# Scans of the first image: products in one PSUM tile, decays in SBUF three steps ahead, and activations taken four in a row from five banks

## Chip, core and metric

The kernel runs on one core of one Trainium2 chip. The metric is the time of one execution on the device in microseconds, as the median of several runs. The engines that matter are TensorE (PE), VectorE (DVE), ScalarE (ACT), GpSimd (POOL) and SyncE (SP), which here only issues DMAs. Each works through its own queue of instructions in order, and semaphores make one wait for another.

## What is computed

Two layers on an input of 4 images with 64 x 64 positions and 128 channels. The first normalises the input and runs a selective state-space layer over each image in three orders (forward, backward, and in 16 interleaved slices). The second is attention with 16 heads of 8 channels, a small feed-forward, and 64 experts, each with its top 8 tokens. The change touches the first layer alone:

```
x, z = split(in_proj(x))                      # 256 channels each
x = silu(causal_conv1d(x, conv_w, conv_b))    # 4 taps
dt_raw, B, C = split(x_proj_w @ x)            # 8, 16, 16 rows
delta = softplus(dt_w @ dt_raw + dt_b)
for each position:                            # the scan, one state for each channel and n < 16
    h = h * exp(delta * A) + (delta * x) * B
    y = sum over n of h * C
y = (y + D * x) * silu(z)
```

## The kernel before

All data is float32. The sequence of an image (4096 positions) is cut into 4 chunks of T = 1024. For an image, an order and a chunk, class Inputs makes what the scan reads, and class Scans scans it. A scan step works on one tile of 128 x 1024: 16 channels by 8 states on the partitions, positions along the row. A chunk has 256 channels by 16 states, so 32 steps, and an image 3 x 4 x 32 = 384.

**Inputs.** For one chunk, `of_chunk` runs these parts, each with a `yield` at which others get their turn:
- cv (L396): projection and convolution in one, 4 groups of 4 matmuls, each group into one PSUM bank of 512 columns; each followed by a Silu on ACT into u (L400)
- xd (L407): two banks of the projection to dt_raw, B and C, copied by ACT (L409)
- dt (L421): four matmuls into four banks, with Softplus on ACT into r (L427), which is delta
- the product of delta and u, for the early chunks, on POOL (L436)
- the results go to DRAM: u, delta, the product, B and C, by DMAs on SP.

`gate` (L352, L358) makes Silu(z) of a quarter of an image in the same way. The `norm` of an image loads and transposes x (L302), copies it (L304), takes statistics on DVE (L307) and normalises (L328). These share three banks: `bank` hands one out and waits, by yielding, while three are held; `leave` gives one back.

**Scans.** Step s of `of_image`: `load(s)` brings delta and du (the product of delta and x, broadcast over the states; one tile serves two steps), B, C and u. delta has three tiles and is loaded by SP, du has four and, for image 0, is loaded from ACT's queue. `exp(s)` (L525) computes the decay exp(delta A) on ACT, and `inputs(s)` (L532) the product of du with B on DVE. `step(s)` runs the scan on DVE (L542), has POOL copy its last column for the next chunk (ends, L544) and, for image 0, multiply with C (hC, L549); for later images DVE does that. `total` (L580) adds over the states on PE, for a group of four steps at a time, and `out` (L596) adds D x on DVE from the one bank `y`.

For image 0 (`alone`) the loads run four steps ahead of the step, the decay one step and the product two. Its decays lie in two PSUM tiles of two banks each; its products in three SBUF tiles. So PSUM's 8 banks go to the decays (4), Inputs (3) and y (1).

**Order of the work around the change.** While image 0 is scanned, the inputs of all four images are made. The order on every engine is the order in which the program issues, set by hand:

```
first = Pace(decays(nc, dirs, ws, inputs), scans.of_image(0, inputs.made, True))
others = Pace(flow(inputs.pieces(range(nb)), 2, 10))
while not first.done:
    others.run(1.2)
    first.run(1.0)
others.rest()
```

`Pace.run(x)` advances its generator to x more yields. A scan step has two yields, so 2.4 yields of the others fall on one. `flow` keeps up to two pieces (a chunk, a gate, a norm) in progress, advances them in turn, and starts another when the last has come 10 yields far. Afterwards the attention of image 0 begins, beside the scans of image 1.

Of the kernel before, what the change touches and what calls it, by code (L numbers as in the profile page):

```python
# [11 lines left out]
F32 = mybir.dt.float32  # L12
AF = mybir.ActivationFunctionType
# [3 lines left out]
P = 128  # L17
# [4 lines left out]
NS = 16  # L22
R = 8
SLICES = 16
ORDERS = {0: (0, 1, 2), 1: (1, 2, 0)}
T = 1024
NC = L // T
# [206 lines left out]
class Inputs:  # L234
# [3 lines left out]
    def __init__(self, tc, ctx, x, w_z, ws, cols, dram, ident):  # L238
        nc = self.nc = tc.nc
        self.x, self.w_z, self.ws, self.cols, self.dram, self.ident = x, w_z, ws, cols, dram, ident  # L240
        const = ctx.enter_context(tc.tile_pool(name="i_const", bufs=1))
        self.big = ctx.enter_context(tc.tile_pool(name="i_big", bufs=1))
        self.piece = ctx.enter_context(tc.tile_pool(name="i_piece", bufs=1))
        self.small = ctx.enter_context(tc.tile_pool(name="i_small", bufs=2))
        self.ps = ctx.enter_context(tc.tile_pool(name="i_ps", bufs=3, space=PSUM))

        group = const.tile([P, 32, 4], F32, name="group")
        nc.gpsimd.memset(group, 0.25)
        nc.gpsimd.affine_select(
            out=group, in_=group, compare_op=ALU.is_ge, fill=0.0,  # L250
            base=0, pattern=[[-4, 32], [0, 4]], channel_multiplier=1,
        )
        nc.gpsimd.affine_select(
            out=group, in_=group, compare_op=ALU.is_ge, fill=0.0,
            base=3, pattern=[[4, 32], [0, 4]], channel_multiplier=-1,
        )
        self.group = group.rearrange("p g r -> p (g r)")
        self.made, self.sz, self.normed, self.sliced, self.gated = {}, {}, {}, {}, {}
        self.held = 0

    def bank(self, name):
        while self.held == 3:
            yield WAIT
        self.held += 1
        return self.ps.tile([P, 512], F32, tag="a", name=name)

    def leave(self):
        self.held -= 1
# [75 lines left out]
    def gate(self, b, g):  # L344
        nc, xn = self.nc, self.normed[b]
        s_g = self.piece.tile([P, 2, T], F32, tag="u", bufs=2, name=f"z_{b}_{g}")
        for m in range(2):
            banks = []
            for i in range(T // 512):
                ps = yield from self.bank(f"z_{b}_{g}_{m}_{i}")  # L350
                at = 3 + g * T + i * 512
                nc.tensor.matmul(  # L352
                    ps, self.w_z[:, m * P : (m + 1) * P], xn[:, at : at + 512], start=True, stop=True,
                )
                banks.append(ps)
            yield
            for i, ps in enumerate(banks):
                nc.scalar.activation(s_g[:, m, i * 512 : (i + 1) * 512], ps, AF.Silu)  # L358
                self.leave()
        yield  # L360
        yield
        nc.sync.dma_start(out=self.sz[b].rearrange("(m p) t -> p m t", p=P)[:, :, g * T : (g + 1) * T], in_=s_g)
        self.gated[b] += 1
        yield

    def of_chunk(self, b, order, c):
# [21 lines left out]

        halves = [slice(g * 512, (g + 1) * 512) for g in range(T // 512)]
        u = self.piece.tile([P, 2, T], F32, tag="u", bufs=2, name=f"u_{key}")  # L390
        for m in range(2):
            bias = w["conv_b"][:, m : m + 1]
            for g, cut in enumerate(halves):
                ps = yield from self.bank(f"cv_{key}_{m}_{g}")
                for k in range(4):
                    nc.tensor.matmul(  # L396
                        ps, w["conv"][:, k, m * P : (m + 1) * P], reads(k, g), start=(k == 0), stop=(k == 3)
                    )
                yield
                nc.scalar.activation(u[:, m, cut], ps, AF.Silu, bias=bias)  # L400
                self.leave()
        yield
        xd = self.piece.tile([X_ROWS, T], F32, tag="xd", name=f"xds_{key}")
# [7 lines left out]
        keep("u", u)  # L411
        yield
        r = self.piece.tile([P, 2, T], F32, tag="r", name=f"r_{key}")
        for m in range(2):
            banks = []
            for g in range(2):
                banks.append((yield from self.bank(f"dt_{key}_{m}_{g}")))
            for g, cut in enumerate(halves):
                at = 32 * (2 * m + g)
                rows = slice(at, at + R)  # L420
                nc.tensor.matmul(banks[g], w["dt"][rows, m, :], xd[rows, cut], start=True, stop=True)  # L421
            if m == 0:
                nc.sync.dma_start(out=made["bc"][0], in_=xd[B_ROW : B_ROW + NS])
                nc.sync.dma_start(out=made["bc"][1], in_=xd[C_ROW : C_ROW + NS])
            yield
            for g, cut in enumerate(halves):
                nc.scalar.activation(  # L427
                    r[:, m, cut], banks[g], AF.Softplus, bias=w["dt_proj_b"][:, m : m + 1]
                )
                self.leave()  # L430
        yield
# [14 lines left out]
class Scans:  # L446
# [24 lines left out]
    def of_image(self, b, made, alone=False):  # L471
# [45 lines left out]
        def exp(s):  # L517
            order, c, k, j = steps[s]
            t = tiles["delta", s]
            if alone:  # L520
                tiles["delta", s] = self.ps.tile([P, T], F32, tag="dA", name=f"dA_{b}_{s}")
            elif j % 2 == 0:
                tiles["delta", s] = self.deep.tile([P, T], F32, tag="dA", bufs=2, name=f"dA_{b}_{s}")
            A = self.ws[order]["A"][:, j % 2, 2 * k + j // 2].unsqueeze(1)
            nc.scalar.activation(tiles["delta", s], t, AF.Exp, scale=A)  # L525

        def inputs(s):
            order, c, k, j = steps[s]
            du = tiles["du", s]
            if alone or j % 2 == 0:  # L530
                tiles["du", s] = self.deep.tile([P, T], F32, tag="dB", bufs=3, name=f"dB_{b}_{s}")
            nc.vector.tensor_mul(tiles["du", s], du, spread[order, c, "B", j % 2])  # L532

        def step(s):
# [8 lines left out]
            if c < NC - 1:  # L543
                nc.gpsimd.tensor_copy(ends[order, c][:, at : at + 1], h[:, T - 1 :])  # L544
            if alone:
                if s + 2 < n:
                    inputs(s + 2)
                tiles["du", s] = self.lone.tile([P, T], F32, tag="hC", bufs=5, name=f"hC_{b}_{s}")
                nc.gpsimd.tensor_mul(tiles["du", s], h, spread[order, c, "C", j % 2])  # L549
                return  # L550
# [81 lines left out]
        if b == 0:  # L632
            for w in self.ws:
                nc.scalar.activation(w["A"], w["A"], AF.Exp)
                nc.vector.tensor_scalar_mul(w["A"], w["A"], -1.0)
        exp(0)
        for s in range(2 if alone else 1):
            inputs(s)
        y = None

        def sums(s):
# [10 lines left out]
        for s in range(n):  # L652
# [7 lines left out]
                y = self.bank.grab(f"y_{b}_{s}")  # L660
            if s + ahead < n:
                load(s + ahead)
            if s + 1 < n:
                exp(s + 1)
                self.did.add("exp")
            if turn in (1, 2):
                sums(s)
# [834 lines left out]
def tile_kernel(tc, ctx, x, in_proj_w, dirs, out_proj_w, attn, gate, weight1, weight2, out):  # L1502
# [15 lines left out]
    with ExitStack() as fill:  # L1518
# [6 lines left out]
        inputs = Inputs(tc, fill, x, w_z, ws, cols, dram, ident)  # L1525
        scans.bank = Bank(fill.enter_context(tc.tile_pool(name="s_bank", bufs=1, space=PSUM)), 1)
        scans.lone = fill.enter_context(tc.tile_pool(name="s_lone", bufs=1))
        scans.ps = fill.enter_context(tc.tile_pool(name="s_ps", bufs=2, space=PSUM))
        with tc.manual_schedule():
            first = Pace(decays(nc, dirs, ws, inputs), scans.of_image(0, inputs.made, True))  # L1530
            others = Pace(flow(inputs.pieces(range(nb)), 2, 10))
            while not first.done:
                others.run(1.2)
                first.run(1.0)
            others.rest()
    bank = scans.bank = Bank(ctx.enter_context(tc.tile_pool(name="bank", bufs=1, space=PSUM)), 1)
# [115 lines left out]
```

## Time and profile before

| what | value |
|---|---|
| median of 3 runs | 11542.6 us (11537.03 to 11542.7) |
| the profiled execution | 11539.8 us, of which the span is 11538.0 us |
| busy in the span: PE, DVE, ACT, POOL | 87%, 71%, 89%, 33% |
| mean granted clock of PE in the span | 0.935 |
| first scan of image 0 starts, last one ends | 113.8 us, 1941.9 us |
| matmul cv (L396), all | 1536 instructions |
| decays of image 0 (L525), mean in 113 to 1824 us | 1117 ns |
| products of image 0 (L532), mean in 113 to 1824 us | 1316 ns |
| hC (L549), all 384 | 976.8 us busy, mean 2544 ns |

A matmul of 128 x 512 in float32 stands in the profile as two instructions, so cv's 768 matmuls are 1536. The lines of the profile name the source line, the engine, the operation and what is written and read; "mean" is that of one instruction, and the time after the bar's second part is the engine's idle time just before, with what ended it. Idle time is put down to the semaphore that is seen last. Where an instruction waits for several semaphores, a separate wait in the sequencer can hide the true cause, and "issue" then stands in its place. A table load (ACT_TABLE_LOAD) is the change of ACT's set of functions, which Exp, Silu and Softplus each need.

### The profile page before, as it was taken

To read this page: it belongs to the slowest core of one execution; us is meant where nothing else is said; L and a number is where in the kernel's file an instruction comes from. 1 tells how busy PE (TensorE), PEld (TensorE's weight loads), DVE (VectorE), ACT (ScalarE), POOL (GpSimd) and SP (SyncE) were. 2 spreads that over 40 slices of the span, in tenths; PEclk is the share of its full clock that TensorE was granted. 3 is DMA by queue.
4 is the path that set the end of the run, shared out by engine and by line. 5 is a ranking of instruction groups with operands and counts; after the bars stand their busy time and mean duration, and the time that the engine had idled before them with its cause. 6 is when DMAs were issued, how large, how long until landed. Compare 5 with 4: busy or idle time off the path is not lost.

```text
span 11538.0 us, 182909 instructions
## 1 busy us (share of the span) xinstructions
PE 10009.7 (87%) x68358; PEld 3314.4 (29%) x68358; DVE 8174.7 (71%) x8379; ACT 10305.7 (89%) x11065; POOL 3770.4 (33%) x3917
## 2 busy tenths in 40 slices
PE   7787784488999889999998898999998999999995
PEld 3233332122222222222222222222222223333323
DVE  5777777788888987998898978988988421111212
ACT  5687784599999999999999999999999999989992
POOL 5776666232322312424333224233332110000000
PEclk8788886799999999999999999999999999999997
DMA  6777777656665665566565656655556332222225
GB/s 188 213 231 204 210 213 202 178 138 154 152 150 146 174 190 138 158 159 149 145 155 148 181 170 161 155 144 144 149 144 170 125 94 71 70 78 83 75 65 184
DMA packets 900977, 1747.50 MB, mean 151 GB/s; under 512 B 203150, under 2 KB 443846, under 8 KB 899830
## 3 DMA queue, kind: packets, MB, share of 16 engines
q1 hardware_dynamic: 764734, 1469.68, 47.0%
q0 software_dynamic: 93856, 156.41, 4.8%
q10 hardware_dynamic: 41496, 109.71, 3.5%
q8 instruction: 537, 8.80, 0.3%
q14 instruction: 354, 2.90, 0.1%
HBM read 1379.76 MB, written 355.47 MB: 150 GB/s over the span
## 4 chain that ended last, share of the span: by engine, by line
PE 34%; ACT 23%; issue 14%; DVE 7%; DMA 6%; POOL 1%; SPq 1%; ACTq 0%; DVEq 0%; POOLq 0%
PE acc L992 20%; ACT e L983 20%; PE s L978 9%; DVE h L542 2%; DMA du<-d_du 1%; DMA delta<-d_delta 1%; ACT dA L525 1%; PE fo L1149 1%; ACT delta L525 1%; PE h L1136 1%; DMA w<-in_L_ffn_weight_dram 1%; DVE dB L532 1%; PE y L580 1%; DMA y<-d_y 0%; DVE du L553 0%
## 5 line engine op out<-in xcount | busy, mean ns | idle before, releaser
L983 ACT ACTIVATE e<-s 128x1024 f32<-128x1024 f32 x8192 | 7778.9, 1106 | 231.1 <-PE s L978 193.2
L992 PE MATMUL acc<-e,val 128*32 128x512 f32 x32768 | 5250.0, 616 | 105.5 <-ACT av L1001 91.6
L978 PE MATMUL s<-qm,key 32*128 32x512 f32 x16384 | 2652.0, 501 | 587.0 <-ACT e L983 556.6
L978 PEld LDWEIGHTS s<-qm,key 32*128 32x128 f32 x16384 | 1013.2, 184 | 4448.6 <-issue 2493.7
L544 POOL COPY ends<-h 128x1 f32<-128x1 f32 x1152 | 1264.9, 1099 | 2501.6 <-DVE h L542 2486.2
L542 DVE TENSOR_TENSOR_SCAN h<-dA,ends,dB 128x1024 f32<-128x1024 f32 x720 | 1687.6, 2344 | 337.2 <-issue 205.7
L532 DVE TENSOR_TENSOR dB<-du,B 128x1024 f32<-128x1024 f32 x960 | 1197.0, 1247 | 408.0 <-PE y L580 221.2
L992 PEld LDWEIGHTS acc<-e,val 128*32 128x32 f32 x32768 | 971.3, 109 | 1603.1 <-issue 788.8
L525 ACT ACTIVATE dA<-delta,A 128x1024 f32<-128x1024 f32 x960 | 1143.4, 1193 | 221.9 <-DVE h L542 131.3
L542 DVE TENSOR_TENSOR_SCAN h<-delta,ends,du 128x1024 f32<-128x1024 f32 x432 | 1012.1, 2343 | 132.1 <-ACT delta L525 65.4
L549 POOL TENSOR_TENSOR hC<-h,C 128x1024 f32<-128x1024 f32 x384 | 976.8, 2544 | 146.8 <-DVE h L542 73.0
L525 ACT ACTIVATE delta<-delta,A 128x1024 f32<-128x1024 f32 x576 | 717.2, 1245 | 0.1
L553 DVE TENSOR_TENSOR du<-h,C 128x1024 f32<-128x1024 f32 x576 | 700.9, 1217 | 0.1
L553 DVE TENSOR_TENSOR dB<-h,C 128x1024 f32<-128x1024 f32 x576 | 700.8, 1217 | 0.0
L532 DVE TENSOR_TENSOR du<-du,B 128x1024 f32<-128x1024 f32 x576 | 690.5, 1199 | 5.3 <-DMA B<-d_bc 5.2
L542 DVE TENSOR_TENSOR_SCAN h<-dA,dB 128x1024 f32<-128x1024 f32 x240 | 548.4, 2285 | 123.1 <-issue 69.8
L1007 POOL DMA_DIRECT2D d_ctx<-av x512 | 260.3, 518 | 1013.9 <-DVE av L1001 645.1
L396 PE MATMUL cv<-xn,conv 128*128 128x512 f32 x1024 | 499.4, 644 | 32.3 <-DVE xn L328 32.3
L574 POOL DMA_DIRECT2D d_du<-x_delta x272 | 157.2, 578 | 1012.1 <-DVE x_delta L573 950.2
L580 PE MATMUL y<-dB,sel 128*32 128x256 f32 x4608 | 376.7, 399 | 9.9 <-DVE xT L1176 6.2
L580 PE MATMUL y<-hC,sel 128*32 128x256 f32 x3072 | 255.5, 467 | 144.7 <-DVE o L596 139.6
L542 DVE TENSOR_TENSOR_SCAN h<-delta,du 128x1024 f32<-128x1024 f32 x144 | 328.8, 2283 | 68.5 <-issue 35.4
(244 smaller groups left out, 7248.8 us busy)
## 6 DMA issues: line engine op xcount, KB each, us to landing
delta<-d_delta SPq DMA_DIRECT2D x768, 512.0 KB
du<-d_du SPq DMA_DIRECT2D x576, 512.0 KB
du<-d_du ACTq DMA_DIRECT2D x192, 512.0 KB
key<-d_q SPq DMA_DIRECT2D x352, 256.0 KB
d_u<-u SPq DMA_DIRECT2D x48, 1024.0 KB
d_delta<-r SPq DMA_DIRECT2D x48, 1024.0 KB
B<-d_bc SPq DMA_DIRECT2D x96, 512.0 KB
C<-d_bc SPq DMA_DIRECT2D x96, 512.0 KB
```

What stands on the lines that cost most here:

```text
L396: nc.tensor.matmul(ps, w["conv"][:, k, m * P : (m + 1) * P], reads(k, g), start=(k == 0), stop=(k == 3))
L525: nc.scalar.activation(tiles["delta", s], t, AF.Exp, scale=A)
L532: nc.vector.tensor_mul(tiles["du", s], du, spread[order, c, "B", j % 2])
L542: nc.vector.tensor_tensor_scan(h, dA, dB, first, ALU.mult, ALU.add)
L544: nc.gpsimd.tensor_copy(ends[order, c][:, at : at + 1], h[:, T - 1 :])
L549: nc.gpsimd.tensor_mul(tiles["du", s], h, spread[order, c, "C", j % 2])
L553: nc.vector.tensor_mul(dB, h, spread[order, c, "C", j % 2])
L580: nc.tensor.matmul(y[32 * g : 32 * g + 32, : T // 4], self.sel[:, j // 2, :], hC[:, 256 * g : 256 * g + 256], start=(j == 0), stop=(j == 3),)
L978: nc.tensor.matmul(s_ps[:, k, :], keys[f"{i // 4}"][rows, cut].bitcast(F32R), queries[j, qb][rows, :].bitcast(F32R), start=True, stop=True,)
L983: nc.scalar.activation(e, s_ps, AF.Exp, scale=1.0 / math.sqrt(D))
L992: nc.tensor.matmul(accs[j, qb][32 * k : 32 * k + 32, :], v[:, k * VW : k * VW + 32], es[i][k // 2][:, k % 2, :], start=(kc == 0), stop=(kc ...
L1007: nc.gpsimd.dma_start(out=self.context[b][h * D : h * D + D, cut], in_=av[32 * k : 32 * k + D, :])
```

## The change

Of image 0's scans: the product of du with B (L532) goes to one PSUM tile of two banks and is made one step ahead, so just before its scan. The decays go to SBUF: for even steps to three tiles of their own, for odd steps in place of delta's tile, as in later images. Three decays are issued ahead instead of one. This leaves five banks for Inputs.

Of Inputs: a batch of four banks is taken at once, for cv, for dt and for a gate. All matmuls of the batch are issued first, and after a further yield (for a chunk) the four activations in a row. A chunk has one yield more, and the others' pace goes from 1.2 to 1.3.

```diff
+BANKS = 5
-        self.ps = ctx.enter_context(tc.tile_pool(name="i_ps", bufs=3, space=PSUM))
+        self.ps = ctx.enter_context(tc.tile_pool(name="i_ps", bufs=BANKS, space=PSUM))
...
+    def banks(self, n, name):
+        while self.held + n > BANKS:
+            yield WAIT
+        self.held += n
+        return [self.ps.tile([P, 512], F32, tag="a", name=f"{name}_{i}") for i in range(n)]
...
     def gate(self, b, g):
+        banks = yield from self.banks(4, f"z_{b}_{g}")
         for m in range(2):
-            banks = []
-            for i in range(T // 512):
-                ps = yield from self.bank(f"z_{b}_{g}_{m}_{i}")
+            for i in range(2):
...
-            yield
-            for i, ps in enumerate(banks):
-                nc.scalar.activation(s_g[:, m, i * 512 : (i + 1) * 512], ps, AF.Silu)
+            yield
+        for m in range(2):
+            for i in range(2):
+                nc.scalar.activation(s_g[:, m, i * 512 : (i + 1) * 512], banks[2 * m + i], AF.Silu)
                 self.leave()
...
+        banks = yield from self.banks(4, f"cv_{key}")
         for m in range(2):
-            bias = w["conv_b"][:, m : m + 1]
-            for g, cut in enumerate(halves):
-                ps = yield from self.bank(f"cv_{key}_{m}_{g}")
+            for g in range(2):
                 for k in range(4):
...
                 yield
-                nc.scalar.activation(u[:, m, cut], ps, AF.Silu, bias=bias)
+        yield
+        for m in range(2):
+            for g, cut in enumerate(halves):
+                nc.scalar.activation(u[:, m, cut], banks[2 * m + g], AF.Silu, bias=w["conv_b"][:, m : m + 1])
                 self.leave()
...
+        banks = yield from self.banks(4, f"dt_{key}")
         for m in range(2):
-            banks = []
-            for g in range(2):
-                banks.append((yield from self.bank(f"dt_{key}_{m}_{g}")))
             for g, cut in enumerate(halves):
...
-            if m == 0:
-                nc.sync.dma_start(out=made["bc"][0], in_=xd[B_ROW : B_ROW + NS])
-                nc.sync.dma_start(out=made["bc"][1], in_=xd[C_ROW : C_ROW + NS])
-            yield
+        nc.sync.dma_start(out=made["bc"][0], in_=xd[B_ROW : B_ROW + NS])
+        nc.sync.dma_start(out=made["bc"][1], in_=xd[C_ROW : C_ROW + NS])
+        yield
+        yield
+        for m in range(2):
             for g, cut in enumerate(halves):
...
         def exp(s):
-            if alone:
-                tiles["delta", s] = self.ps.tile([P, T], F32, tag="dA", name=f"dA_{b}_{s}")
-            elif j % 2 == 0:
-                tiles["delta", s] = self.deep.tile([P, T], F32, tag="dA", bufs=2, name=f"dA_{b}_{s}")
+            if j % 2 == 0:
+                tag, bufs = ("dB", 3) if alone else ("dA", 2)
+                tiles["delta", s] = self.deep.tile([P, T], F32, tag=tag, bufs=bufs, name=f"dA_{b}_{s}")
...
         def inputs(s):
-            if alone or j % 2 == 0:
+            if alone:
+                tiles["du", s] = self.ps.tile([P, T], F32, tag="dB", name=f"dB_{b}_{s}")
+            elif j % 2 == 0:
...
             if alone:
-                if s + 2 < n:
-                    inputs(s + 2)
+                if s + 1 < n:
+                    inputs(s + 1)
...
-        exp(0)
-        for s in range(2 if alone else 1):
-            inputs(s)
+        further = 3 if alone else 1
+        for s in range(further):
+            exp(s)
+        inputs(0)
...
-            if s + 1 < n:
-                exp(s + 1)
+            if s + further < n:
+                exp(s + further)
...
-        scans.ps = fill.enter_context(tc.tile_pool(name="s_ps", bufs=2, space=PSUM))
+        scans.ps = fill.enter_context(tc.tile_pool(name="s_ps", bufs=1, space=PSUM))
...
-                others.run(1.2)
+                others.run(1.3)
```

More of the change, by code (lines that the diff above doesn't have):

```diff
@@ L259, in __init__ @@
         self.held = 0
+    def banks(self, n, name):
[3 more added lines that the diff above has]
+        return [self.ps.tile([P, 512], F32, tag="a", name=f"{name}_{i}") for i in range(n)]
     def bank(self, name):
[L262 to L265, printed above, removed]
+        return (yield from self.banks(1, name))[0]
     def leave(self):
@@ L346, in gate @@
         s_g = self.piece.tile([P, 2, T], F32, tag="u", bufs=2, name=f"z_{b}_{g}")
+        banks = yield from self.banks(4, f"z_{b}_{g}")
         for m in range(2):
[L348 to L350 removed]
+            for i in range(2):
                 at = 3 + g * T + i * 512
                 nc.tensor.matmul(
[L353 removed]
+                    banks[2 * m + i], self.w_z[:, m * P : (m + 1) * P], xn[:, at : at + 512], start=True, stop=True,
                 )
[L355 removed]
             yield
[L357 to L358 removed]
+        for m in range(2):
+            for i in range(2):
+                nc.scalar.activation(s_g[:, m, i * 512 : (i + 1) * 512], banks[2 * m + i], AF.Silu)
                 self.leave()
@@ L390, in of_chunk @@
         u = self.piece.tile([P, 2, T], F32, tag="u", bufs=2, name=f"u_{key}")
+        banks = yield from self.banks(4, f"cv_{key}")
         for m in range(2):
-            bias = w["conv_b"][:, m : m + 1]
-            for g, cut in enumerate(halves):
-                ps = yield from self.bank(f"cv_{key}_{m}_{g}")
+            for g in range(2):
                 for k in range(4):
                     nc.tensor.matmul(
-                        ps, w["conv"][:, k, m * P : (m + 1) * P], reads(k, g), start=(k == 0), stop=(k == 3)
+                        banks[2 * m + g], w["conv"][:, k, m * P : (m + 1) * P], reads(k, g), start=(k == 0), stop=(k == 3)
                     )
                 yield
-                nc.scalar.activation(u[:, m, cut], ps, AF.Silu, bias=bias)
+        yield
+        for m in range(2):
+            for g, cut in enumerate(halves):
+                nc.scalar.activation(u[:, m, cut], banks[2 * m + g], AF.Silu, bias=w["conv_b"][:, m : m + 1])
                 self.leave()
@@ L420, in of_chunk @@
                 rows = slice(at, at + R)
-                nc.tensor.matmul(banks[g], w["dt"][rows, m, :], xd[rows, cut], start=True, stop=True)
-            if m == 0:
-                nc.sync.dma_start(out=made["bc"][0], in_=xd[B_ROW : B_ROW + NS])
-                nc.sync.dma_start(out=made["bc"][1], in_=xd[C_ROW : C_ROW + NS])
-            yield
+                nc.tensor.matmul(banks[2 * m + g], w["dt"][rows, m, :], xd[rows, cut], start=True, stop=True)
+        nc.sync.dma_start(out=made["bc"][0], in_=xd[B_ROW : B_ROW + NS])
[3 more added lines that the diff above has]
+        for m in range(2):
             for g, cut in enumerate(halves):
                 nc.scalar.activation(
-                    r[:, m, cut], banks[g], AF.Softplus, bias=w["dt_proj_b"][:, m : m + 1]
+                    r[:, m, cut], banks[2 * m + g], AF.Softplus, bias=w["dt_proj_b"][:, m : m + 1]
                 )
```

## Prediction

> **What bounds the kernel now.** I looked for the stage that the change touches before asking what any instruction costs. All edited lines run while image 0 is scanned; in the trace its 384 scan steps (L542) run from 113.8 to 1941.9 us, 1828 us or 4.76 us a step. The view of windows splits that into the part in which other images' inputs are made beside it, and the tail in which the scans run alone.
>
> ```profile
> core 0: us, PE busy (x) PEld busy (x) DVE busy (x) ACT busy (x) POOL busy (x), PEclk, DMA share, GB/s
> 113.00:1824.00 1711.00, 1388.28 (x5238) 541.55 (x5238) 1318.77 (x845) 1338.36 (x1374) 1240.14 (x682) 0.84 0.75 216
> 1836.00:1942.00 106.00, 26.72 (x232) 11.93 (x232) 106.00 (x69) 32.42 (x29) 93.90 (x30) 0.56 0.69 153
> ```
>
> No engine is full in the first part; DVE is full in the tail. So in the first part something waits for something in turn. The groups of that window name it (busy, mean of one, then idle before them):
>
> ```profile
> L542 DVE TENSOR_TENSOR_SCAN h<-dA,ends,dB 128x1024 f32<-128x1024 f32 x256 | 600.4, 2345 | 254.4 <-issue 187.2 <-POOL hC L549 39.5 <-POOL ends L544 19.2
> L525 ACT ACT_TABLE_LOAD x227 | 291.2, 1283 | 23.8 <-DMA delta<-d_delta 11.5 <-DMA du<-d_du 4.4 <-DMA d_y<-o 3.7
> ...
> L542 DVE TENSOR_TENSOR_SCAN h<-dA,dB 128x1024 f32<-128x1024 f32 x96 | 219.4, 2285 | 90.6 <-issue 66.1 <-POOL ends L544 12.8 <-POOL hC L549 8.5
> ...
> L400 ACT ACT_TABLE_LOAD x136 | 174.5, 1283 | 69.7 <-PE cv L396 49.2 <-issue 16.4 <-DMA d_du<-u 2.0
> ...
> L427 ACT ACT_TABLE_LOAD x60 | 77.0, 1283 | 3.1 <-issue 2.1
> ...
> L358 ACT ACT_TABLE_LOAD x31 | 39.8, 1283 | 0.6
> ```
>
> DVE idles 254.4 + 90.6 = 345.0 us in front of the scans, nearly all of its 392 us idle. "issue", hC and ends are poor names for the cause. The timeline shows it:
>
> ```profile
> 917.47 1.28 ACT L525 ACT_TABLE_LOAD   x1
> ...
> 918.76 1.12 ACT L525 ACTIVATE dA<-delta,A 128x1024 f32<-128x1024 f32 x1
> ...
> 919.90 1.28 ACT L358 ACT_TABLE_LOAD   x1
> 920.32 2.35 DVE L542 TENSOR_TENSOR_SCAN h<-dA,ends,dB 128x1024 f32<-128x1024 f32 x1 [1.72 <-issue]
> ```
>
> The decay ends at 919.88 and the scan starts 0.44 us later. Pairing the n-th decay with the n-th scan, 344.6 us of the 345 end with a decay. The decays have two PSUM tiles, so decay s+1 cannot start before scan s-1 ends; it then has 1.2 us (product) + 2.3 us (scan s), and one Silu between costs 1.28 + 0.69 + 1.28 + 1.12 = 4.37 us.
>
> What comes next is in the waits and in the tail:
>
> ```profile
> PE xt L302 <- DMA x<-in_x_dram: 90.9, 12, 17.9
> ...
> PE y L580 <- DVE o L596: 66.7, 21, 12.6
> PE dt L421 <- ACT r L427: 64.9, 36, 4.0
> ...
> DVE stats L307 <- ACT xn L304: 37.3, 16, 7.6
> ```
>
> ```profile
> 1866.42 1.19 DVE L532 TENSOR_TENSOR dB<-du,B 128x1024 f32<-128x1024 f32 x1
> ...
> 1866.64 3.17 POOL L549 TENSOR_TENSOR hC<-h,C 128x1024 f32<-128x1024 f32 x1 [0.66 <-DVE h L542]
> ...
> 1867.53 2.34 DVE L542 TENSOR_TENSOR_SCAN h<-dA,ends,dB 128x1024 f32<-128x1024 f32 x1
> 1869.79 1.19 DVE L532 TENSOR_TENSOR dB<-du,B 128x1024 f32<-128x1024 f32 x1
> ```
>
> PE is 81% busy in the first part, with idle time that other causes set. DVE's own step is 1.11 (1866.42 to 1867.53) + 2.26 = 3.37 us, and the closing operation (L596, 0.49 us) every fourth step.
>
> [...] The trace has the 1283 ns; the decay follows 1.29 us after the load's start and the load 0.02 us after its forerunner, so I count 1.28 us a switch. [...] hC takes 3.17 us beside a product in the tail, 2.35 us beside a scan. [...] The dependent pair L119, L120 starts 0.71 us apart (1999.35, 2000.06), L120 and its independent follower 0.61. [...] The granted mean is 0.84 at 81% busy and 0.56 at 25%.
>
> **The change part by part.**
>
> *Decays three steps ahead, in SBUF.* Decay s+3 is issued at step s, so a decay may be late by about three steps before DVE notices. The worst pair of batches, Silu and Softplus (each 1.28 + 4 x 0.69 + 1.28 = 5.3 us) with two decays, is 13 us against some 11. The 345.0 us go, apart from what is priced below. The decay itself costs more in SBUF: later images' rows give 1.25 us against 1.12, 384 x 0.13 = 50 us of ACT, hidden while ACT has that idle time (below).
>
> *Fewer table loads.* Now 227 + 136 + 60 + 31 = 454, or 582 us. Afterwards 48 Silu batches, 48 Softplus batches and 16 gate batches, at most two loads each: 224. Counting yields, a few batches adjoin: 221. That takes 233 x 1.283 = 299 us from ACT: 1338 - 299 + 50 = 1089 us. ACT stops being a candidate for the bound.
>
> *Products in one PSUM tile, one step ahead.* Each scan directly follows the product that it reads: +0.10 us x 384 = 38 us on DVE. A write to PSUM by DVE is not in the trace. [...] ScalarE's 1.12 against 1.25 us in favour of PSUM, taken whole for DVE, -50 us. I take 0, since scans from PSUM and SBUF decays take the same (2285 ns here, 2283 ns for h<-delta,du of later images). If the overwrite of the tile also waits for the scan in front, another 38 us.
>
> *delta's tile is held until the scan.* Odd decays are written in place, so the load for pair p+2 waits for scan 2p-1 instead of its decay. SP stands there, with the stores, the us loads and the others' x loads and keeps queued behind it. One turn of the three tiles is six steps: load, wait in ACT's queue, a table load and decay (2.4), two scans with the products (5.9), SP's issue (0.6). Counting SP's bytes against its packets, such loads land after 5.7 us in the median, 10.5 at the 95th percentile. At 4.2 us a step, 25.2 - 8.9 = 16.3 us remain for load and queue: hidden in most turns.
>
> *Four banks in a row out of five.* PE can start a batch's first group in the fifth bank and then needs ACT's activations of the batch before. Only one such batch fits, so batches follow one another strictly, 48 + 48 + 16 = 112 of them. The dt waits for banks (64.9) go. In exchange xd waits for Silus that now start late: between 0 and a load and three Silus, 3.3 us, less what of the other piece lies between; I take 1.25 us x 48 = 60.
>
> *Pace 1.3.* A chunk has one yield more. By the yields, the others end at scan step 361 of 384; now 353. So 23 steps are left alone, at 3.37 + 0.10 + 0.12 = 3.6 us: 83 us.
>
> **The sum.** DVE alone would need 1828 - 345 + 38 = 1521 us. PE for the others' part: matmuls of 512 columns start 0.43 us apart at the full clock (LDWEIGHTS of cv at 899.84 and 900.27), 2432 x 0.43 = 1046, y 215, xt 24: 1285 us, against 1388 now. I take about the middle, 1335. To it come waits that stay: x loads 91, xn 30, xd on u 19, dt on xds 15, small ones 3, together 158, and the 60 above: 1553 us, 4.30 us a step. PE and DVE are tied within a few steps (y needs the products with C, o needs y, one bank), so the longer one ends: 1553 + 83 = 1636, 192 us less than 1828. From the profiled execution's 11539.8 us this gives 11348; the median of the runs is 2.8 us higher, so 11350. Later stages shift as they are.
>
> **The rivals.**
>
> *PE takes over (the forecast), 192 us off.* For it: 81% busy already, and 4.21 us a step in the best 16 steps, PE 94% busy. Its range is PE at the full clock without the xd waits, 1285 + 158, so DVE's 1521 ends: 307 off; to PE as slow as now with all waits and 2.5 us at each xd: 1388 + 158 + 120 = 1666, 79 off.
>
> *DVE's own floor, 307 us off, 11235.* For it: POOL and ACT have room. Against: POOL. Its ends and hC need 3.45 us a step, and 26 products u (2.65 us) fall in the first 97 steps: 404 us against DVE's 349.
>
> *The delta ring binds.* If load and queue average 18 us, a step is (18 + 8.9)/6 = 4.5 us, the stage 1728: 100 off, 11443. Against: 5.7 us median.
>
> *Slower: PE stands at each hand-over of the banks.* 112 batches in series; every wait of PE adds to 1553. From 192/112 = 1.7 us a batch on, nothing is gained; at 3.0 us (a load and most of three activations, uncovered) it is 336 - 192 = 144 us slower, 11694. For it: only one spare bank, and three now serve finer grains. Against: cv's first group (8 x 0.43 = 3.4 us) runs in that bank meanwhile, and a decay's delay no longer reaches DVE.
>
> **How the numbers follow.** PE takes over 0.53, DVE floor 0.14, delta ring 0.17, slower 0.11, and 0.05 that the gains and losses cancel. The range reaches from the floor (11235, 11240 taken) to 11500, which takes in the ring at 19 us. Within 0.2% (23 us; about what a measurement of this kernel tells from no change): 0.05; slower 0.11; faster 0.84.
>
> **What would show it.** Right: idle before L542 falls from 345 to below 80 us; table loads number about 221; PE is above 88% busy with a clock above 0.84 in the first part; the last scan ends near 1750. DVE's product-to-scan distance in the tail is 1.2 instead of 1.11 us. Wrong: PE under 80% busy with waits on u or r in front of cv, xd and dt (the bank rival); ACT idle before L525 on delta loads (the ring); scans still late by decays; DVE products longer than 1.2 us.

## The result, and the profile after

| | before | after |
|---|---|---|
| median (lowest to highest) | 11539.82 us (11534.12 to 11542.7), 4 runs | 11420.67 us (11410.54 to 11439.44), 4 runs |
| ratio after/before | | 0.9899, 95% interval 0.9882 to 0.9916 |
| the profiled execution, and its span | 11539.8, 11538.0 us | 11419.52, 11417.8 us |
| first scan of image 0 starts, last ends | 113.8, 1942.0 us | 107.2, 1814.0 us |
| that stage | 1828.2 us | 1706.7 us |
| table loads of ACT in it | 455 | 222 |
| busy in it: PE, DVE, ACT, POOL | 1419, 1429, 1376, 1337 us | 1293, 1577, 1072, 1350 us |

The change takes 119 us off, 1.0%. The stage accounts for it: 121.5 us shorter. The forecast was 11350 us with a range of 11240 to 11500, so direction and range hold and the gain is 119 instead of 192 us.

In the changed kernel the scan is L547, the decay L528, the product L537, hC L554, ends L549, y L585, o L601; of Inputs, Silu into u is L405, Softplus into r L431, xd L412, cv L398. First the windows of after, the part with the others' inputs and then the tail (columns as in the forecast):

```profile
core 0: us, PE busy (x) PEld busy (x) DVE busy (x) ACT busy (x) POOL busy (x), PEclk, DMA share, GB/s
107.20:1740.00 1632.80, 1275.02 (x5349) 509.60 (x5349) 1504.88 (x879) 1050.21 (x1160) 1286.92 (x695) 0.87 0.81 234
1740.00:1814.00 74.00, 18.03 (x161) 8.17 (x161) 71.81 (x49) 21.33 (x20) 62.58 (x19) 0.55 0.54 122
```

DVE is now 92% busy (1504.88 of 1632.80), against 77% before. PE, which was to become the bound, is 78% busy. But DVE's busy time is not all work, as the groups of the stage show (busy, mean of one in ns, then idle before them and what ended it):

```profile
L554 POOL TENSOR_TENSOR hC<-h,C 128x1024 f32<-128x1024 f32 x383 | 983.5, 2569 | 210.4 <-PE y L585 111.6 <-issue 57.4 <-DVE h L547 33.6
L537 DVE TENSOR_TENSOR dB<-du,B 128x1024 f32<-128x1024 f32 x384 | 610.9, 1591 | 23.8 <-DMA du<-d_du 9.6 <-DMA B<-d_bc 1.3
...
L547 DVE TENSOR_TENSOR_SCAN h<-dA,ends,dB 128x1024 f32<-128x1024 f32 x144 | 337.8, 2346 | 20.6 <-ACT dA L528 3.3
L547 DVE TENSOR_TENSOR_SCAN h<-delta,ends,dB 128x1024 f32<-128x1024 f32 x144 | 336.8, 2339 | 15.9 <-ACT delta L528 6.7 <-DVE dB L537 1.0
...
L528 ACT ACTIVATE dA<-delta,A 128x1024 f32<-128x1024 f32 x191 | 219.0, 1147 | 332.0 <-DMA delta<-d_delta 294.5 <-DVE dB L537 14.8 <-DVE h L547 9.8
```

The idle time in front of the scans has shrunk from 345 to 54 us (two groups with 9 us each are left out here); in 19.1 us of it the decay came last. But a product's mean is 1591 ns, where the first part of before had 1316:

```profile
L532 DVE TENSOR_TENSOR dB<-du,B 128x1024 f32<-128x1024 f32 x353 | 464.7, 1316 | 11.9 <-DMA B<-d_bc 7.2 <-DMA du<-d_du 4.7
```

It has not become more work: the median is 1.23 us (1.20 before). 82 of the 384 took over 1.5 us, and what these spent above 1.2 us adds up to 139 us (before: 31 of them, 36 us). All 82 began while POOL was at work: 69, with 115 us, beside an hC, and 13, with 24 us, beside POOL's product of delta and u. Each ends 1.09 us after that instruction of POOL (1.087 to 1.095). The 292 products that began with no POOL instruction under way took 1.235 us at most, so the 1.09 us are nearly a whole product that comes after POOL's instruction. In the profile such a wait has no line of its own: it is counted as duration. I call these products held; "port" in the expectations below is a name for this hold. Why POOL's instruction has this effect was not shown.

Why does hC run just then? The timeline of after, around one held product, and three lines of the tail:

```profile
994.97 1.15 ACT L528 ACTIVATE dA<-delta,A 128x1024 f32<-128x1024 f32 x1 [6.33 <-DMA delta<-d_delta]
996.13 1.28 ACT L405 ACT_TABLE_LOAD   x1
...
998.17 5.54 PE L412 MATMUL xd<-u,w_x 128*104 128x512 f32 x8 [8.15 <-ACT u L405]
...
1002.40 2.35 DVE L547 TENSOR_TENSOR_SCAN h<-delta,ends,dB 128x1024 f32<-128x1024 f32 x1 [2.58 <-ACT delta L528]
1003.64 1.07 PE L585 MATMUL y<-hC,sel 128*32 128x256 f32 x16
1004.45 2.38 POOL L554 TENSOR_TENSOR hC<-h,C 128x1024 f32<-128x1024 f32 x1 [10.31 <-issue]
1004.78 3.13 DVE L537 TENSOR_TENSOR dB<-du,B 128x1024 f32<-128x1024 f32 x1
...
1745.00 2.35 DVE L547 TENSOR_TENSOR_SCAN h<-dA,ends,dB 128x1024 f32<-128x1024 f32 x1
1747.38 1.23 DVE L537 TENSOR_TENSOR dB<-du,B 128x1024 f32<-128x1024 f32 x1
1748.75 2.35 DVE L547 TENSOR_TENSOR_SCAN h<-delta,ends,dB 128x1024 f32<-128x1024 f32 x1
```

Read it downwards. A decay on ACT waits 6.33 us for a load of delta (by the chain of waits it landed 14.2 us after its issue). The Silu batch stands behind it in ACT's queue, so xd on PE waits 8.15 us for u. y stands behind xd on PE, and until y has read a tile of hC, POOL has no tile for the next one: it waits 10.31 us ("issue" again stands for it, but it ends as y's matmuls run). Then hC starts 0.33 us ahead of a product and holds it for 1.9 us. So DVE, with its decays far ahead, still pays for a late ACT, along ACT, PE and POOL. The waits of after give the totals for the same links (us, times, longest):

```profile
ACT dA L528 <- DMA delta<-d_delta: 260.0, 55, 13.4
...
POOL hC L554 <- PE y L585: 111.6, 43, 8.4
...
PE xd L412 <- ACT u L405: 103.8, 23, 26.1
...
PE xt L306 <- DMA x<-in_x_dram: 88.3, 12, 15.2
...
DVE stats L311 <- ACT xn L308: 49.8, 15, 9.5
```

xd's wait on u was 19 us before, hC's on y 52 us. The wait of hC is not all due to xd's: during its 111.6 us PE is at work for 106, 76 of them on matmuls of Inputs that stand ahead of y in its queue. That xd's wait came first, as in the timeline, is shown for this one place.

### The profile page after: what moved, and what is told of

Its sections match the earlier page's. It is cut to its first block, busy times and chain, and to the rows that moved or that the text cites. A ratio compares the mean times of both kernels' runs of the same rounds, so it can differ in the third digit from the quotient of the medians.

```text
span 11417.8 us, 183032 instructions
## 1 busy us (share of the span) xinstructions
PE 9875.8 (86%) x68358; PEld 3273.8 (29%) x68358; DVE 8319.4 (73%) x8379; ACT 9990.1 (87%) x10828; POOL 3815.4 (33%) x3917
## 4 chain that ended last, share of the span: by engine, by line
PE 37%; ACT 23%; issue 14%; DVE 14%; DMA 11%; POOL 1%; SPq 1%; ACTq 0%; DVEq 0%; POOLq 0%
PE acc L998 21%; ACT e L989 19%; PE s L984 10%; DVE h L547 6%; DMA delta<-d_delta 4%; DVE dB L537 2%; DMA du<-d_du 2%; PE cv L398 1%; ACT dA L528 1%; PE y L585 1%; ACT delta L528 1%; PE fo L1155 1%; PE h L1142 1%; DMA B<-d_bc 1%; PE xd L412 1%
## 5 line engine op out<-in xcount | busy, mean ns | idle before, releaser
L549 POOL COPY ends<-h 128x1 f32<-128x1 f32 x1152 | 1298.8, 1129 | 2274.5 <-DVE h L547 2265.9
L537 DVE TENSOR_TENSOR dB<-du,B 128x1024 f32<-128x1024 f32 x960 | 1306.5, 1361 | 426.9 <-PE y L585 225.1
L547 DVE TENSOR_TENSOR_SCAN h<-dA,ends,dB 128x1024 f32<-128x1024 f32 x576 | 1350.6, 2345 | 100.4 <-ACT dA L528 57.5
L528 ACT ACTIVATE dA<-delta,A 128x1024 f32<-128x1024 f32 x768 | 934.4, 1217 | 461.4 <-DMA delta<-d_delta 422.8
L547 DVE TENSOR_TENSOR_SCAN h<-delta,ends,du 128x1024 f32<-128x1024 f32 x432 | 1012.5, 2344 | 124.3 <-ACT delta L528 62.3
L554 POOL TENSOR_TENSOR hC<-h,C 128x1024 f32<-128x1024 f32 x384 | 985.8, 2569 | 210.8 <-PE y L585 111.6
L528 ACT ACTIVATE delta<-delta,A 128x1024 f32<-128x1024 f32 x768 | 936.7, 1220 | 7.1 <-issue 2.0
L537 DVE TENSOR_TENSOR du<-du,B 128x1024 f32<-128x1024 f32 x576 | 690.7, 1199 | 6.4 <-DMA B<-d_bc 6.3
L398 PE MATMUL cv<-xn,conv 128*128 128x512 f32 x1024 | 476.5, 620 | 37.8 <-DVE xn L332 25.6
L547 DVE TENSOR_TENSOR_SCAN h<-dA,dB 128x1024 f32<-128x1024 f32 x192 | 438.7, 2285 | 41.3 <-ACT dA L528 30.1
L585 PE MATMUL y<-dB,sel 128*32 128x256 f32 x4608 | 379.3, 401 | 8.1 <-DVE xT L1182 5.2
L547 DVE TENSOR_TENSOR_SCAN h<-delta,du 128x1024 f32<-128x1024 f32 x144 | 328.8, 2283 | 67.3 <-issue 34.9
L585 PE MATMUL y<-du,sel 128*32 128x256 f32 x4608 | 364.3, 388 | 0.0
```

What stands on the lines that cost most here:

```text
L398: nc.tensor.matmul(banks[2 * m + g], w["conv"][:, k, m * P : (m + 1) * P], reads(k, g), start=(k == 0), stop=(k == 3))
L547: nc.vector.tensor_tensor_scan(h, dA, dB, first, ALU.mult, ALU.add)
L585: nc.tensor.matmul(y[32 * g : 32 * g + 32, : T // 4], self.sel[:, j // 2, :], hC[:, 256 * g : 256 * g + 256], start=(j == 0), stop=(j == 3),)
```

## The experiments

In the order of the questions. Times are medians, each with its ratio to the kernel before on the same chip (that one: 11538.69 us beside e1 to e4, 11540.96 beside e5 to e8, 11552.23 beside e9 to e12). As that kernel moves by up to 14 us between the groups, a smaller difference between runs of two groups says nothing. "Late decays" is DVE's idle time ended by a decay, "held" the time above 1.2 us of all products over 1.5 us, both in the stage. Table loads are counted here from the program's start to the end of the stage, 4 to 6 of them ahead of the first scan in runs with loads. In summary:

| run | us | stage | loads to its end | late decays | held | hC waits for y |
|---|---|---|---|---|---|---|
| before | 11539.8 | 1828.2 | 461 | 344.6 | 35.8 | 52.3 |
| after | 11420.7 | 1706.7 | 226 | 19.1 | 139.4 | 111.6 |
| e1_one_tile | 11556.9 | 1848.8 | 463 | 58.8 | 220.3 | 348.6 |
| e2_two_tiles | 11548.8 | 1830.6 | 463 | 5.1 | 170.6 | 304.4 |
| e4_before_next | 11553.2 | 1844.9 | 463 | 320.9 | 46.6 | 49.2 |
| e9_before_noload | 11425.9 | 1700.6 | 1 | 163.9 | 61.4 | 67.4 |
| e10_one_tile_noload | 11443.7 | 1733.9 | 3 | 10.0 | 169.4 | 202.7 |
| e5_one_decay | 11423.9 | 1714.7 | 226 | 116.2 | 51.7 | 53.3 |
| e3_hc7 | 11397.7 | 1692.5 | 226 | 44.3 | 76.9 | 4.5 |
| e8_ends_dve_hc7 | 11396.1 | 1685.4 | 226 | 41.8 | 72.1 | 24.7 |
| e7_delta5 | 11425.2 | 1713.4 | 226 | 20.5 | 139.1 | 100.2 |
| e6_two_taps | 11382.8 | 1680.0 | 226 | 20.1 | 106.8 | 63.7 |
| e11_norm_ahead | 11359.9 | 1648.5 | 222 | 15.8 | 118.8 | 122.3 |
| e12_norm_u | 11385.7 | 1656.4 | 222 | 12.2 | 48.3 | 103.1 |

**The lead of the decays alone.** The scans of after with the Inputs of before: three banks, one Silu or Softplus at a time, pace 1.2.

```diff
...
-                tiles["delta", s] = self.ps.tile([P, T], F32, tag="dA", name=f"dA_{b}_{s}")
...
+            if j % 2 == 0:
+                tag, bufs = ("dB", 3) if alone else ("dA", 2)
...
+                tiles["du", s] = self.ps.tile([P, T], F32, tag="dB", name=f"dB_{b}_{s}")
...
-                if s + 2 < n:
-                    inputs(s + 2)
+                if s + 1 < n:
+                    inputs(s + 1)
...
-            if s + 1 < n:
-                exp(s + 1)
+            if s + further < n:
+                exp(s + further)
...
```

> The changed kernel's scans (decays in SBUF three steps ahead, products in one PSUM tile one step ahead) with the Inputs of the kernel before (three banks, activations after each bank, pace 1.2). Theory 'order' (the shortfall comes from each product standing right before its scan in one tile): the scans' tail, where DVE runs alone, has 3.81 us a step as in the changed kernel; decays still no longer late (idle before the scans under 60 us); 454 table loads; about 11430 to 11480 us, since ACT keeps its loads but no longer holds DVE up. Theory 'the four-in-a-row batches bring the gain': close to the time before, 11520 to 11540.

Measured 11556.88 us, ratio 1.0019 [1.0012, 1.0027]. Half the change gains nothing at all: a clear miss of the order theory, and above the 11520 to 11540 us of the other one too. The groups of its stage, in the first 1740 us:

```profile
L550 POOL TENSOR_TENSOR hC<-h,C 128x1024 f32<-128x1024 f32 x333 | 823.1, 2476 | 367.4 <-PE y L581 319.3 <-issue 42.9 <-DVE h L543 4.8
L533 DVE TENSOR_TENSOR dB<-du,B 128x1024 f32<-128x1024 f32 x335 | 616.8, 1841 | 45.6 <-DMA du<-d_du 31.5 <-DMA B<-d_bc 3.0
```

Late decays fall from 345 to 59 us, and held products rise from 36 to 220, with a mean of 1841 ns. hC waits 319 us for y. Most of DVE's wait has not gone, it has been put into the duration of another instruction.

**The order within a DVE step.** If the product right ahead of its scan costs the gain, two PSUM tiles for the products, made two ahead, must give it back:

```diff
-                if s + 1 < n:
-                    inputs(s + 1)
+                if s + 2 < n:
+                    inputs(s + 2)
...
-        scans.ps = fill.enter_context(tc.tile_pool(name="s_ps", bufs=1, space=PSUM))
+        scans.ps = fill.enter_context(tc.tile_pool(name="s_ps", bufs=2, space=PSUM))
```

> As the run e1, but the products have two PSUM tiles and are made two steps ahead, so a scan never follows its own product. Theory 'order': 3.50 us a step in the tail instead of 3.81, product to scan 1.11 us instead of 1.36, and 60 to 120 us less than e1. Theory 'PE takes over' (the forecast): DVE's own step does not set the time, so within 20 us of e1.

Measured 11548.79 us, ratio 1.001 [1.0001, 1.0019]: 8 us less than e1. And the reverse, the kernel before with its products in SBUF but made one ahead:

```diff
-                if s + 2 < n:
-                    inputs(s + 2)
+                if s + 1 < n:
+                    inputs(s + 1)
```

> The kernel before with its products (still in three SBUF tiles) made one step ahead instead of two: the order alone, without PSUM. If being right behind its product costs the scan what the pair L119, L120 shows, product to scan is 1.21 us in the tail instead of 1.11; if it costs as much as in the changed kernel, 1.36, and PSUM has no share. Scan to product stays 2.26. The total moves by less than 40 us, since late decays hide most of it.

Measured 11553.22 us, ratio 1.0012 [1.0003, 1.0022]: 14 us above the kernel before. The timeline of its tail, to be set beside that of after:

```profile
1902.40 2.35 DVE L542 TENSOR_TENSOR_SCAN h<-dA,ends,dB 128x1024 f32<-128x1024 f32 x1
1904.67 1.20 DVE L532 TENSOR_TENSOR dB<-du,B 128x1024 f32<-128x1024 f32 x1
1906.00 2.35 DVE L542 TENSOR_TENSOR_SCAN h<-dA,ends,dB 128x1024 f32<-128x1024 f32 x1
```

Scan to product is 2.27 us here and 2.38 in after; product to its own scan 1.33 here and 1.37 in after, against 1.11 in the kernel before, where the scan after a product reads an earlier one. Four steps with their closing operation take 13.98 us in before, 14.64 in e4, 14.54 in e2 and 15.23 in after. So order costs 0.66 and PSUM 0.56 us per four steps, and together, 1.25, it is 120 us over 384 steps. That is a cost in DVE's own need; yet taking away about half of it (e2, 66 us by this count) moves the time by 8 us. The trace of e2 shows where the rest went: late decays fall by 54 us more and held products by 50, but the products now wait 153 us for loads of du, against 25 in e1. ACT's queue issues these loads. So in e2, too, the waits went elsewhere, which speaks against DVE's own need as what sets the time.

**The table loads alone.** The kernel before, with Exp in place of Silu and Softplus in Inputs, so that ACT has no set to change (one of the three lines is shown). The values of u, delta and z's gate differ; sizes and instructions stay.

```diff
-                nc.scalar.activation(u[:, m, cut], ps, AF.Silu, bias=bias)
+                nc.scalar.activation(u[:, m, cut], ps, AF.Exp, bias=bias)
```

> The kernel before with Exp in place of Silu and Softplus for all inputs (the values are others), so that ACT never changes its table during image 0's scans; nothing else moves: decays still one ahead in PSUM, three banks. Theory 'loads' (the change gains by the 235 table loads fewer, 301 us of ACT, and not by the decays' lead): the 454 loads are gone, so at least as fast as the changed kernel, 11300 to 11430. Theory 'lead' (decays must run ahead): decays are late as often, 11480 us or more.

Measured 11425.85 us, ratio 0.9892 [0.9877, 0.9906]: the gain of the whole change, with decays one ahead, products in SBUF and three banks. Scans wait less for their decays; late decays fall from 345 to 164 us. Of the two groups that had 254.4 and 90.6 us of idle time before, the first, in the first 1740 us:

```profile
L542 DVE TENSOR_TENSOR_SCAN h<-dA,ends,dB 128x1024 f32<-128x1024 f32 x266 | 622.6, 2341 | 122.2 <-issue 98.8 <-ACT dA L525 10.1 <-POOL hC L549 7.0
```

The same edit on e1:

> The run e1 (the changed kernel's scans beside the Inputs of before) with Exp in place of Silu and Softplus (other values), so no table loads. Theory 'loads': what e1 lacked against the changed kernel comes back, 11380 to 11440, POOL's wait on y from 349 us to under 120. Theory 'banks' (three banks instead of five keep PE and ACT in step): little changes, 11500 to 11560. Against e9, both without loads: theory 'order' says that e10 is slower than e9, by up to 120 us, since its DVE step is 0.31 us longer.

Measured 11443.72 us, ratio 0.9907 [0.9891, 0.9924]. It is 113 us better than e1 (129 by the two ratios), and 18 us slower than e9: without loads too, the rearranged scans gain nothing. The mean product of e10 shows where it stays: 1667 ns. hC still waits 203 us for y, where the loads theory had under 120. During these 203 us PE is at work for 195, 152 of them on matmuls of Inputs ahead of y.

**The batches without the lead.** After, with decays one step ahead:

```diff
-        further = 3 if alone else 1
+        further = 1
```

> The changed kernel with the decay one step ahead again (everything else stays: batches of four, five banks, decays in SBUF, one PSUM product tile). Theory 'both are needed' (late decays stop DVE unless they run ahead, and PE with ACT sets the pace unless the table loads go): a batch of 5.3 us delays each decay behind it, idle before the scans by decays above 200 us, 11500 us or more. Theory 'the batches alone give the gain': idle by decays under 100 us and within 25 us of the changed kernel (11396 to 11446).

Measured 11423.92 us, ratio 0.9894 [0.9878, 0.9911], as after. The groups of e5 in its first 1740 us:

```profile
L554 POOL TENSOR_TENSOR hC<-h,C 128x1024 f32<-128x1024 f32 x362 | 920.5, 2543 | 92.5 <-PE y L585 53.3 <-DVE h L547 37.2 <-PE dt L424 0.8
L537 DVE TENSOR_TENSOR dB<-du,B 128x1024 f32<-128x1024 f32 x363 | 498.3, 1373 | 22.6 <-DMA du<-d_du 6.9 <-DMA B<-d_bc 3.2
L547 DVE TENSOR_TENSOR_SCAN h<-dA,ends,dB 128x1024 f32<-128x1024 f32 x134 | 314.3, 2346 | 76.6 <-ACT dA L528 62.8 <-ACT r L431 0.5
...
L528 ACT ACTIVATE dA<-delta,A 128x1024 f32<-128x1024 f32 x183 | 209.3, 1143 | 83.7 <-DMA delta<-d_delta 82.9
```

Decays are late again (116 us), but ACT waits for delta loads 83 us before the even decays in these 1740 us, where after has 266. Over the stage, xd's wait on u falls from 104 to 33 us, and held products from 139 to 52. Late and held together are 168 us here and 158 in after. Loads run four steps ahead; a decay three ahead follows its load by one step, 4.4 us in the mean (1706.7/384), and then ACT stands with the Silu batch behind it. So the three steps' lead brings nothing: what DVE gains at the scan it loses at the product. What e5 keeps, it keeps together: batches with fewer loads, five banks, the pace of 1.3. No run has the batches, banks and pace with the loads left in, so that the loads bring the gain of the changed kernel too is inferred from e9.

**POOL's tiles.** After, with seven tiles for hC (room from one tile each of B and C; e7 below has the same saving):

```diff
-                tiles["du", s] = self.lone.tile([P, T], F32, tag="hC", bufs=5, name=f"hC_{b}_{s}")
+                tiles["du", s] = self.lone.tile([P, T], F32, tag="hC", bufs=7, name=f"hC_{b}_{s}")
```

> The changed kernel with seven buffers for hC instead of five (room from one B and one C tile of image 0, which keep four in all). Theory 'port' (POOL stands for y on PE, so its hC then overlaps a product [...]): the wait of hC on y falls from 112 us to under 40, products over 1.5 us from 82 to under 45, and the time by 40 to 90 us. Theory 'PE takes over': POOL's wait only moves, the time stays within 20 us of the changed kernel. Theory 'ring' (delta loads): no change either.

Measured 11397.72 us, ratio 0.9876 [0.9861, 0.989]: 23 us less than after, where 40 to 90 were expected. The groups of e3 in its stage:

```profile
L557 POOL TENSOR_TENSOR hC<-h,C 128x1024 f32<-128x1024 f32 x384 | 991.7, 2583 | 71.0 <-DVE h L550 57.1 <-PE y L588 4.5 <-DVE cos_ry L64 4.0
L540 DVE TENSOR_TENSOR dB<-du,B 128x1024 f32<-128x1024 f32 x384 | 548.9, 1429 | 35.3 <-DMA du<-d_du 21.4 <-DMA B<-d_bc 1.3
```

Held products nearly halve (from 139 to 77 us), so the path from y over hC's tiles to the product is shown; of the 62 us, 25 come back as late decays. Then the copy of the last column taken from POOL to DVE, between product and scan, on top of e3:

```diff
-            if c < NC - 1:
+            if c < NC - 1 and not alone:
...
+                if c < NC - 1:
+                    nc.vector.tensor_copy(ends[order, c][:, at : at + 1], h[:, T - 1 :])
```

> The run e3 (seven hC buffers) with the copy of the last column for image 0 moved from POOL to DVE, between a product and its scan, where DVE stands 0.24 us for the product anyway. Theory 'port and order': the copy costs DVE nothing there, POOL starts hC at once and has about 1.1 us a step less, so products over 1.5 us fall under 30 and the time by 20 to 60 us against e3 (11340 to 11380). Theory 'PE takes over': within 15 us of e3.

Measured 11396.05 us, ratio 0.987 [0.9856, 0.9885]: no different from e3. POOL's 307 us of ends weren't the cause of what is left of the held products.

**The delta ring.** After, with five tiles for delta instead of three:

```diff
+                if alone and name == "delta" and s // 2 % 5 > 2:
+                    t = self.lone.tile([P, T], F32, tag="delta", bufs=2, name=f"{name}_{b}_{s}")
...
```

> The changed kernel with five delta tiles for image 0 instead of three, so that a load no longer waits for a scan. Theory 'ring' (delta loads hold ACT, and through ACT's Silus PE's xd and y): ACT's wait for delta falls from 316 us to under 100, xd's wait for u (104 us on PE) by half, and the time by 30 to 80 us. Rival: ACT has idle time to spare, so its wait moves elsewhere, and the time stays within 15 us.

Measured 11425.18 us, ratio 0.9897 [0.9882, 0.9912], as after; ACT still waits 255.9 us for delta before its even decays. So delta's tiles alone don't keep the loads back. SP, which issues them in order, waits in front of other DMAs of its queue: in after for scans before the delta loads (165 us), for o before the loads of u (262), and for ACT's u before its store (180). With five tiles the first is gone, and the second is 360 us. Whether SP's queue is what makes the loads late was not tested, nor were loads more than four steps ahead.

**PE's work.** After, with two of the four taps of the convolution left out, which takes 241 us of PE's busy time. A single run:

```diff
-                for k in range(4):
+                for k in range(2):
```

> The changed kernel with two of the convolution's four taps left out, so PE has 768 matmul instructions less (330 us at 0.43 us each) and nothing else changes. Theory 'PE takes over' (the forecast: PE's order with ACT's activations in it sets the pace of the stage): the stage falls by 100 us or more, to 1600 us or less, POOL's wait on y under 50 us. Theory 'DVE sets it by order and port': the stage stays within 50 us of 1707.

Measured 11382.83 us (no interval): 38 us less than after, the stage 27 us. The windows:

```profile
107.00:1700.00 1593.00, 1031.22 (x4604) 389.21 (x4604) 1461.89 (x871) 1044.43 (x1157) 1292.51 (x692) 0.78 0.83 238
```

PE is 65% busy and waits where it worked: its wait on u in front of xd is 204 us. PE's work is not the bound.

**What is left.** In after PE waits 88 us for the x loads of norm, and DVE 50 us behind them. After, with up to three tiles of x loaded ahead and statistics one yield later (the same saving of B and C as in e3):

```diff
+                xs.append(self.piece.tile([P, 8, C], F32, tag="x_g", bufs=3, name=f"x_{b}_{g}"))
+                nc.sync.dma_start(out=xs[g], in_=xin[:, g * 8 : g * 8 + 8, :])
...
+        for g in range(3):
+            bring()
+        yield
+        yield
...
+                yield
                 nc.vector.bn_stats(stats[:, 2 * g + k, :], cut)
+            bring()
```

> The changed kernel with the x tiles of a norm loaded up to three ahead (three x tiles instead of one; room from one B and one C tile). Theory 'norm' (of the 1707 us, 3 x 50 us are lost where PE, ACT and DVE stand in turn for an x load): PE's wait on x falls from 88 us to under 30, DVE's statistics wait from 50 to under 25, and the time by 30 to 80 us against the changed kernel. Rival: the stage is held by DVE's order, port and ACT, so within 15 us.

Measured 11359.93 us, ratio 0.9834 [0.982, 0.9849]: 61 us less than after, the best of all. The waits of e11 that answer to those of after:

```profile
PE xt L317 <- DMA x<-in_x_dram: 40.5, 3, 15.4
...
DVE stats L323 <- ACT xn L319: 23.8, 5, 10.6
```

DVE's wait for statistics falls by 26 us. But the edit's further yields also spread Inputs over the scans: their last activation ends at step 383 of 384 (362 in after), and no tail is left. Which part of the 61 us is whose was not separated. Held products stay at 119 us. So I also moved the early products of delta and u from POOL to DVE, on top of e11:

```diff
-            by = nc.vector if (b, order, c) == (0, orders(0)[0], 0) else nc.gpsimd
+            by = nc.vector
```

> The run e11 with the 26 early products of delta and u on DVE instead of POOL (two were there already). Theory 'port' (in the first 100 steps, POOL is late by these 2.65 us each and then holds up DVE's products): products over 1.5 us in the first 100 steps lose some 50 us of excess, DVE gains 30 us of work, so 10 to 40 us less than e11. Rival: DVE is the bound there and the 30 us show as a loss.

Measured 11385.73 us (11360.67 to 11393.86), ratio 0.9853 [0.9839, 0.9868]. Held products fall to 48 us, but the moved products wait 46.5 us on DVE. Not better than e11.

## Why the prediction was right, and where not

The direction was right, and the time lies in the range because the range was wide: it reached from some 300 to some 40 us off. The mechanism that gave its middle, PE taking over, did not come. What was left of DVE's 345 us after two costs, one missing from the sum and one too small in it, fell inside by luck. Of the signs named, the idle time before the scans (54 us), the loads (222) and the clock (0.87) came out; PE above 88% busy, the end near 1750 us and 1.2 us from product to scan did not.

*The decays' 345 us go.* Right for the scans (19.1 us are left). But the forecast counted them as DVE's gain. Most of it was not to be had there: e1, which takes the same step alone, gains nothing, and e5, which omits the lead, loses nothing.

*Fewer table loads: 221, 299 us of ACT, "ACT stops being a candidate for the bound".* The count is right (222). ACT is busy for 1050 us in the first part against 1089: the decays in SBUF cost 0.03 us more each (1.147 against 1.117 us), 12 us in place of 50. The role given to it is the first wrong step: the sum puts nothing on the loads and 345 us on the lead. e9 gets the whole gain from the loads alone, and e5 from batches without the lead. In the kernel before, the loads stand in front of the decays: without them late decays fall by 181 us. In the changed kernel, the links from ACT on are u for xd, xd ahead of y, y for hC, hC beside the product. That a shorter ACT queue shortens this loop fits e5, but only its last links, from y on, were taken alone (e3). e9 takes away twice as many loads as the change and gains no more, which suggests that below some number they no longer set the time; where, was not measured.

*The order's +0.10 us and nothing for PSUM: 38 us.* The mis-sized term: measured in the tail, 1.25 us per four steps, 120 us. The order costs 0.22 us in three of four steps (in the fourth the closing operation stands between: product to closing operation 1.12 us and on to the scan 0.48 in e4, 1.11 and 0.49 before), where I took 0.10 from a pair of other operations; PSUM costs 0.14 a step, where I took 0 and held a gain of 0.13, ACT's 1.12 against 1.25 us, to be possible. In the time it shows for less: e2 gives back about half of it and moves the time by 8 us.

*PE takes over: 1335 + 158 + 60.* The second wrong step. PE's busy time came out lower than said (1275 us in the first part; the forecast's 0.43 us a matmul was read at a granted clock of 1.00, at 899 to 901 us of before), and its idle time higher: 358 us, where 218 were counted. xd waits 104 us for u (19 and 60 counted), and y 60 us for o, a wait that the forecast shows with 67 us and leaves out of its sum. PE was 78% busy where the forecast asked for 88, and e6, with 241 us less work on PE, gains 27 us in the stage. So PE's work and waits can't be added to a bound here: when the work goes, the waits grow (xd's on u from 104 to 204 us in e6).

*What DVE pays instead.* Per stage, with its own step from the tail times 96 groups of four. This is an estimate: the last row is what remains, and as DVE's other work is 41 us before and 45 after, the 1462 are some 20 us too many.

| us | before | after | e5 |
|---|---|---|---|
| own steps | 1342 | 1462 | 1462 |
| late decays | 345 | 19 | 116 |
| held products | 36 | 139 | 52 |
| waits of statistics | 38 | 50 | 51 |
| products that wait for a load | 7 | 4 | 3 |
| DVE's other work and the rest | 60 | 33 | 31 |
| stage | 1828 | 1707 | 1715 |

So of the 345 us, 19 stay, 103 come back as held products and 120 as a longer step; the other rows take 18 us off, which leaves 121 us of gain. I had named "DVE products longer than 1.2 us" as a sign against the forecast, and had put no price on it.

*The rivals.* DVE's own floor fell: its 307 us need POOL out of the way, and POOL, the argument held against it in the forecast, is what was seen, though not as a full engine (79% busy) but as one that holds DVE's products up. The delta ring gives a time close to the measured one (11443), but e7 shows that its tiles alone aren't the cause; the waits for delta, 316 us with those before table loads, come with a decay issued one step after its load (81 us in e5). Of the bank hand-overs the sign was seen, PE under 80% busy with a wait of xd on u; but no run takes banks and batches apart, and the kernel did not get slower. In e10 xd waits only 27 us for u, and y is late all the same, behind other matmuls in PE's queue; whether another order of PE's work would help was not tried. Nor was the pace changed alone: Inputs end 22 steps before the scans in after and 31 in before.

*The tail.* It was put at 23 steps and 83 us. After the last activation of Inputs 22 steps are left, which take 93 us; DVE's own step in it is 3.81 us, where 3.6 was counted.

## What to carry to other kernels

When several engines wait in turn and none is full, ask which one's queue the loop runs through, and shorten that (here ACT's table loads by batches); running one engine ahead only moved the wait to the next place here. Look for waits inside durations: the products' mean rose from 1316 to 1591 ns while their median stayed near 1.2 us, and all of the excess lay beside POOL's work. And test a proposed bound by taking its work away before adding up its waits.

## What was not expected of the hardware

- A result read by the next DVE instruction cost 0.22 us more in the pair product and scan (1.33 in e4 against 1.11 us before, from start to start), against 0.10 us (0.71 against 0.61) in the pair that the forecast used.
- A VectorE product of 128 x 1024 written to PSUM took 1.23 us against 1.20 to SBUF, and started 0.11 us later after a scan (2.38 against 2.27 us).
- A decay of 128 x 1024 written to SBUF took 1.147 us against 1.117 to PSUM here, not the 1.25 us of later images' rows.
- Exp in place of Silu and Softplus (e9) takes 455 loads, some 584 us of ACT, out of the stage and shortens it by 127.6 us; the change, with half of that (233 loads), by 121.5 us.
